# A two-layer graph network on one core: the first layer's two projections as one job of 15 products, with its small steps placed one by one

## The chip, the core and the metric

The kernel runs on one core of a Trainium2 chip. The metric is the device time of the whole kernel in microseconds (us), as the median of several runs. Beside the runs there is one profiled execution, from which all views of the profile come.

## The reference

`x` is (128 graphs, 64 nodes, 768 features) in float32, `adj` a mask of (128, 64, 64). There are two layers, and each ends in a layer norm over features with its input added. Cut to what matters:

```python
# layer 0: 12 heads of 64
h    = einsum('bnd,ade->bane', x, W)                     # one 768 x 768 projection
th   = tanh(h)
attn = leaky(th . w_src + swap(th . w_dst))              # one number a node and head each
attn = softmax(where(adj, attn, -999))
feat = elu(einsum('banm,bame->bane', attn, h) + b)
gate = sigmoid(x @ H_w.T + H_b)                          # a second 768 x 768 projection
x    = layernorm(x + gate * feat + (1 - gate) * x)
# layer 1: 6 heads of 128
q, k, v = x @ Wq + bq, x @ Wk + bk, x @ Wv + bv
ctx  = softmax(where(adj, q k^T / sqrt(128), -9e15)) v
x    = layernorm(x + ctx @ Wf + bf)
```

All 8192 rows of x pass the six 768 x 768 projections. Everything is computed in float32.

## The kernel before

**Tiles.** 128 rows (two graphs) are a tile, two tiles a pair; there are 32 pairs. `t0 = 2p` and `t1 = 2p + 1` are the tiles of pair p. Layer 0 and the values v of layer 1 are done pair by pair in a first stage (up to about 1480 us), queries, keys, attention and output in a second, by groups of two pairs. The second stage is the same before and after but for where in SBUF the weights of q and k lie.

**Products with fewer multiplications.** In the first stage a projection of a pair is a `Job` (L247): rows, inner dimension and columns are halved, and seven block products (1 to 7) replace eight, at the price of block sums. A product is three matmuls of 128 x 128 weights (rows of x, transposed) on 384 columns of the weight matrix (L270). Blocks of x are summed on GpSimd (`x_sums`, L1086, by `block_sums`, L232: four sums of 128x384), the weights' blocks once on VectorE (`weight_sums`, L213). `way_out` (L279) takes results out of PSUM: the first on a place of the output is a copy on ScalarE (h and v, L850, L879) or an addition of the bias on VectorE (gate, L866), later ones are additions on VectorE (L851, L867, L880). The second stage has the same idea with 15 products of 256-wide blocks (`WIDE`, L70), where the inner dimension and the columns are cut in three and the rows in two.

**PSUM.** There are eight banks of 128 x 512: three with tag `y`, three `z`, two `m`. A job's products use `y` and `z`; transposes and attention use `m`. A bank is given out again in turn, and its next matmul waits for the last read of what it held.

**Order.** The order is written out by hand. `TURN` (L121) lists the 21 products that PE does in a turn of a pair: `h` and `g` (gate) of pair p, `v` of pair p - 1, and `u`, the rest of v of pair p - 2. `FIRST`, `SECOND` and `THIRD_AT` are for the first three pairs, `LAST` for the end, where the products of q come in. All other work is attached to positions in the turn by `at` and `was` (L1119, L1123). `step` (L305) issues a product, then the `way_out` of the product before it; then come the acts of that position. Each engine works its own list in this order and waits only for data and buffers. SyncE starts all DMA transfers, in program order too.

**The steps of a tile in layer 0**, with their lines: `products` (tanh on ScalarE, times w_dst on VectorE, times w_src on GpSimd, L888 to L890); `terms` (sums over a head on VectorE, L897, then the dst terms go to DRAM as a 128 x 12 block, L899, and come back broadcast to 64 partitions, L902, as `dd`); `with_bias` (b is added to h on GpSimd, L913, then halves of h are sent across to other partitions by DMA as `hx`, L918); `logits` (L926), `leaky`, `masked` (L942 to L949), `exps`; `probs_by_nodes` (transposes through `m`, L966), `attend` (small matmuls, L987, with a column of ones for the sum), `features` (L1003, L1004); `gate_tanh` (ScalarE), `residual` (gate times x on GpSimd, L1017), `elu1`, `gated` (L1022 to L1029); `stats`, `normed` (the layer norm, L310: moments on VectorE, a power on GpSimd at L322, scale on ScalarE at L327, then the row spill to DRAM); `by_features` (transposes of the result), `value_sums` and `v`.

**Beside it** the generator `sum_weights` (L346) makes the sums of weight blocks for the second stage, from DRAM to DRAM: loads of 128x256, additions on GpSimd (L366), a store. Each item of a turn moves it on by one or two steps.

Of the kernel before, what the change touches and what calls it, by code (L numbers as in the profile page):

```python
# [24 lines left out]
EP = E0 + 2  # L25
# [21 lines left out]
WOVEN = [  # L47
    (0, 1), (1, 1), (0, 2), (1, 2), (0, 6), (1, 6), (0, 5),
    (0, 7), (1, 5), (1, 7), (0, 4), (0, 3), (1, 4), (1, 3),
]  # L50

FIRST = ["h1", "h2", "h5", "h6", "g1", "h7", "g2", "h4", "g6", "g5", "g7", "h3", "g3"]

FIRST_AT = {3: 0, 6: 10, 8: 3, 11: 8, 12: 12, 13: 12, 14: 13, 15: 14, 16: 14, 17: 14, 18: 15, 19: 19, 20: 19}
SECOND = [
    "h1", "G4", "h2", "g1", "g2", "h6", "h5", "h7", "g6", "h4",
    "g5", "g7", "h3", "g4", "g3", "H1", "v1", "v2", "v6", "v5", "v7", "H2",
]  # L60
SECOND_AT = {11: 10, 12: 13, 13: 13, 14: 14, 15: 14, 16: 15, 17: 16, 18: 18, 19: 19, 20: 20}
SECOND_OLD = {
    7.5: 12, 0: 7, 1: 8, 2: 8, 3: 9, 4: 10, 5: 11, 6: 12, 7: 12, 8: 13, 9: 14, 11: 15, 12: 15, 15: 16, 16: 17, 19: 19,
}

# [26 lines left out]
    ["u4", "u3"]  # L95
    + [f"q{n}" for n in (0, 1, 2, 3, 4, 5, 6, 8, 7, 9, 10, 11, 12)]
    + ["v1", "v2", "v6", "q13", "v5", "v7", "q14", "v4", "v3"]
)
LAST_AT = {7.5: 8, 3: 3, 4: 4, 5: 5, 6: 6, 7: 7, 8: 9, 9: 10, 11: 12, 12: 13, 15: 15, 16: 17, 19: 18}
# [21 lines left out]
TURN = [  # L121
    "h1", "h2", "u4", "u3", "h6", "g1", "h5", "h7", "g2", "g6", "h4",
    "h3", "g5", "g7", "v1", "v2", "g4", "v6", "g3", "v5", "v7",
]

THIRD_AT = {pos: max(int(pos) - 2, 0) for pos in [*range(len(TURN)), 7.5]}
TURNS = {
    0: (FIRST, FIRST_AT, {}),
    1: (SECOND, SECOND_AT, SECOND_OLD),
    2: (TURN[2:], THIRD_AT, THIRD_AT),  # L130
}
# [3 lines left out]
def kernel(  # L135
# [9 lines left out]
    hwT: bass.AP,  # L145
# [33 lines left out]
    dst_d = [dram.tile([P, H0], F32, name=f"dstd_{t}") for t in range(2 * NP)]  # L179
# [164 lines left out]
    bias_c = {k: load_cols(src, f"b{k}_c") for k, src in (("q", bq), ("k", bk), ("v", bv))}  # L344

    def sum_weights(pool):  # L346

        for key, src in (("q", wq), ("k", wk), ("f", wf)):
            for n, (_, blocks, *_) in enumerate(WIDE):
                if blocks[0][2] > 0 and len(blocks) == 1:  # L350
                    continue
                for kc in range(2):

                    def block(k, f):
                        r0 = (2 * k + kc) * P
                        return src[r0 : r0 + P, f * W2 : (f + 1) * W2]

                    acc = pool.tile([P, W2], F32, tag="wacc", name=f"wacc_{key}{n}_{kc}", bufs=1)
                    nc.sync.dma_start(out=acc, in_=block(*blocks[0][:2]))
                    for k, f, sign in blocks[1:]:  # L360
                        t = pool.tile([P, W2], F32, tag="wadd", name=f"wadd_{key}{n}_{kc}_{k}{f}", bufs=1)
                        nc.sync.dma_start(out=t, in_=block(k, f))
                        yield
                        yield
                        yield
                        G.tensor_tensor(acc, acc, t, ALU.add if sign > 0 else ALU.subtract)  # L366
                    if blocks[0][2] < 0:
                        assert len(blocks) == 1
                        yield
                        yield  # L370
                        yield
                        G.tensor_scalar(acc, acc, -1.0, None, ALU.mult)
                    yield
                    yield
                    nc.sync.dma_start(out=wide_d[key][n][:, kc, :], in_=acc)
                    yield
                    yield

    def wide_place(key, n):
        flat = weights[key].rearrange("p b k f -> p (b k f)")  # L380
        at = PLACE[n] * 2 * W2
        return flat[:, at : at + 2 * W2].rearrange("p (k f) -> p k f", k=2)
# [373 lines left out]
    with ExitStack() as ph, ExitStack() as ph_r:  # L756
# [13 lines left out]
        def load_x(p):  # L770
            ts = []
            for i in range(PAIR):
                t = sb.tile([P, D], F32, tag="x", name=f"x_{2 * p + i}")
                nc.sync.dma_start(out=t, in_=x[p, :, i, :])
                ts.append(t)
            return ts
# [14 lines left out]
        xTs[0] = sbr.tile([P, KC, PAIR * P], F32, tag="xT", name="xT_0")  # L791
        w0_w = weights["q"] = wpool.tile([P, 7, HK, HALF], F32, tag="wa", name="w0_wq")
        for kh, blocks in ((0, (B11,)), (1, (B21, T3, B22))):
            rows = slice(kh * HK, (kh + 1) * HK)
            nc.sync.dma_start(out=xTs[0][:, rows, :], in_=xT[0][:, rows, :])
            for block in blocks:
                load_block(w0, w0_w, block)
        hb_bc = load_rows(sbr, hb, D, "hb_bc")
        b01_bc = load_rows(sb, b0, E0, "b01_bc")
        hw_w = weights["k"] = load_weight(hwT, "wb", "hw_wk", (B11, B21, T3, B22))  # L800
# [3 lines left out]
        A[0], x_steps = sums_of(G, sbr, "sx", xTs[0], "x0")  # L804
        all_of(x_steps)
        t1, t2, t4, t3 = weight_sums(V, w0_w)
        all_of((t1, t2, t3, t4))
# [21 lines left out]
        def new_h(t):  # L829
            h = sb.tile([P, H0, EP], F32, tag="h", name=f"h_{t}", bufs=3)  # L830
            G.memset(h[:, :, E0:], 1.0)
            return h

        h_of = per_tile("h", new_h)
        gate_of = per_tile("gate", lambda t: sb.tile([P, D], F32, tag="gate", name=f"gate_{t}", bufs=3))
        v_of = per_tile("v", lambda t: sb.tile([P, D], F32, tag="v", name=f"v_{t}"))


        def h_job(p):
            def at(m, n):  # L840
                return h_of(p, m)[:, n * J0 : (n + 1) * J0, :E0]

            def as_heads(b):
                return b.rearrange("p (j e) -> p j e", e=E0)

            return token_job(
                f"h{p}",
                A[p],
                w0_w,
                lambda mn, b: S.copy(at(*mn), as_heads(b)),  # L850
                lambda mn, b: V.tensor_tensor(at(*mn), as_heads(b), at(*mn), ALU.add),  # L851
                lambda b: S.copy(at(1, 0), as_heads(b)),
            )

        def gate_job(p):
            def at(m, n):
                return gate_of(p, m)[:, n * HALF : (n + 1) * HALF]

            def bias(n):
                return hb_bc[:, n * HALF : (n + 1) * HALF]  # L860

            return token_job(
                f"g{p}",
                A[p],
                hw_w,
                lambda mn, b: V.tensor_tensor(at(*mn), b, bias(mn[1]), ALU.add),  # L866
                lambda mn, b: V.tensor_tensor(at(*mn), b, at(*mn), ALU.add),  # L867
                lambda b: V.tensor_tensor(at(1, 0), b, bias(0), ALU.add),
            )
# [14 lines left out]
        def products(t):  # L884

            h = st[t]["h"]
            th = sbr.tile([P, 2, D], F32, tag="th", name=f"th_{t}")
            S.activation(th[:, 1, :].rearrange("p (a e) -> p a e", e=E0), h[:, :, :E0], AF.Tanh)  # L888
            V.tensor_tensor(th[:, 0, :], th[:, 1, :], wsd[:, 0, :], ALU.mult)  # L889
            G.tensor_tensor(th[:, 1, :], th[:, 1, :], wsd[:, 1, :], ALU.mult)  # L890
            st[t]["th"] = th

        def terms(t):

            th = st[t].pop("th")
            sd = small.tile([P, 2 * H0], F32, tag="sd", name=f"sd_{t}")
            V.tensor_reduce(sd, th.rearrange("p s (a e) -> p (s a) e", e=E0), AX.X, ALU.add)  # L897
            st[t]["sd"] = sd
            nc.sync.dma_start(out=dst_d[t], in_=sd[:, :H0])  # L899
            dd = work(f"dd_{t}")  # L900
            for g in range(2):
                nc.sync.dma_start(  # L902
                    out=dd[g * N : (g + 1) * N, :],
                    in_=dst_d[t][g * N : (g + 1) * N, :]
                    .rearrange("m a -> (m a)")
                    .partition_broadcast(N),
# [3 lines left out]
        def with_bias(t):  # L910

            h = st[t]["h"]
# [3 lines left out]

            hx = sb.tile([P, J0, EP], F32, tag="hx", name=f"hx_{t}")
# [4 lines left out]
        def logits(t):  # L922
            sd, dd = st[t].pop("sd"), st[t].pop("dd")
            att = work(f"att_{t}")
            att3 = att.rearrange("p (a m) -> p a m", m=N)
            V.tensor_tensor(  # L926
                att3,
                dd.rearrange("p (m a) -> p a m", a=H0),
                sd[:, H0:].unsqueeze(2).to_broadcast([P, H0, N]),
# [50 lines left out]
        def attend(t):  # L980
            pT, h, hx = st[t].pop("pT"), st[t].pop("h"), st[t].pop("hx")
# [32 lines left out]
        def residual(t):  # L1014

            xp = st[t]["x"]
            G.tensor_tensor(xp, st[t]["gate"], xp, ALU.mult)  # L1017
# [6 lines left out]
        def gated(t):  # L1024

            ex, gate, u = (st[t].pop(k) for k in ("ex", "gate", "x"))
            V.scalar_tensor_tensor(ex, gate, 4.0, ex, ALU.add, ALU.mult)
            x1 = sb.tile([P, D], F32, tag="x1", name=f"x1_{t}")
# [4 lines left out]
        def stats(t):  # L1033
            next(st[t]["norm"])
# [327 lines left out]
```

## Time and profile before

| | |
|---|---|
| median of 3 runs | 2881.39 us (2880.11 to 2882.06) |
| profiled execution, span | 2888.2 us |
| granted TensorE clock, mean | 0.998 |
| VectorE, ScalarE, GpSimd busy | 67%, 37%, 45% of the span |
| DMA moved | 348.73 MB, mean 121 GB/s |
| first matmul | 7.67 us after the start |
| last pair's products of h end, queries begin | about 1480 us |

In the profile PE is TensorE's matmuls, PEld its weight loads, DVE VectorE, ACT ScalarE, POOL GpSimd and SP SyncE. A group's row has busy time and the mean duration of one instruction, then the idle time of the engine in front of it and what ended most of that. A row of waits has the waiting engine and what it waited for, then total us, times and the longest. A float32 matmul on 64 columns or more is in the records as two.

### The profile page before, as it was taken

How to read it: one execution, taken by the hardware profiler on the slowest of the kernel's cores; microseconds unless marked ns; L12 is line 12 of the kernel's file. 1: busy time of each engine (PE TensorE's matmuls, PEld its weight loads, DVE VectorE, ACT ScalarE, POOL GpSimd, SP SyncE). 2: the span in 40 equal slices, each digit the busy share in tenths (PEclk: the TensorE clock that was granted, in tenths of full speed). 3: DMA queues.
4: the chain of work that ended last, by engine and by line, in shares of the span. 5: the costliest groups of instructions: out<-in, count | busy, mean ns of one | idle time of the engine just before them, and what ended most of it. 6: DMA issues, size and time to landing. Idle time of an engine off the chain costs nothing.

```text
span 2888.2 us, 47874 instructions
## 1 busy us (share of the span) xinstructions
PE 2840.2 (98%) x18252; PEld 2075.9 (72%) x18252; DVE 1924.9 (67%) x3203; ACT 1061.2 (37%) x1896; POOL 1303.5 (45%) x1253
## 2 busy tenths in 40 slices
PE   8999999999999999999999999999999999999998
PEld 4565556666566666666668888888888888888886
DVE  7888888887888888777763545555544555554556
ACT  2444444444444444444433223333222333322332
POOL 3444445454444544343343445343545443444534
PEclk9999999999999999999999999999999999999999
DMA  5444444444445444333353434432323333233432
GB/s 182 132 154 145 140 150 143 159 148 151 141 142 162 135 155 142 105 116 108 121 195 96 122 91 111 111 92 84 77 79 111 111 104 95 68 84 94 111 88 74
DMA packets 322068, 348.73 MB, mean 121 GB/s; under 512 B 147888, under 2 KB 247216, under 8 KB 321840
## 3 DMA queue, kind: packets, MB, share of 16 engines
q1 hardware_dynamic: 321840, 345.66, 39.7%
q8 instruction: 146, 2.39, 0.4%
q14 instruction: 82, 0.67, 0.1%
HBM read 198.48 MB, written 122.29 MB: 111 GB/s over the span
## 4 chain that ended last, share of the span: by engine, by line
PE 80%; DVE 9%; DMA 4%; ACT 3%; issue 2%; POOL 1%; SPq 1%; POOLq 0%; DVEq 0%; ACTq 0%
PE z_k L447 9%; PE z_o L494 9%; PE z_q L447 8%; PE y_h L270 6%; PE y_g L270 6%; PE y_k L447 6%; PE y_o L494 6%; PE y_q L447 5%; PE y_v L270 5%; PE z_h L270 4%; PE z_v L270 3%; PE z_g L270 2%; PE cp L634 2%; PE sp L550 2%; PE x_g L270 2%
## 5 line engine op out<-in xcount | busy, mean ns | idle before, releaser
L574 ACT ACTIVATE sc<-sc 128x512 f32<-128x512 f32 x48 | 30.7, 639 | 616.9 <-DVE sc L571 616.9
L695 POOL TENSOR_TENSOR y<-y,bf_bc 128x768 f32<-128x768 f32 x64 | 114.7, 1817 | 295.1 <-DMA y<-x1d 265.5
L507 DVE TENSOR_TENSOR y<-y,z_o 128x256 f32<-128x256 f32 x320 | 127.4, 417 | 140.0 <-PE z_o L494 139.9
L494 PE MATMUL z_o<-wf,so 128*128 128x256 f32 x896 | 215.8, 383 | 2.3 <-DVE y L507 1.2
L447 PE MATMUL z_q<-xs,w_wq 128*128 128x256 f32 x896 | 213.5, 381 | 1.0 <-POOL xs L411 0.9
L411 POOL TENSOR_TENSOR so<-ctxT 128x256 f32<-128x256 f32 x224 | 160.5, 737 | 89.8 <-PE y_o L494 44.0
L447 PE MATMUL z_k<-xs,hw_wk 128*128 128x256 f32 x840 | 200.0, 381 | 0.0
L447 PEld LDWEIGHTS z_q<-xs,w_wq 128*128 128x128 f32 x896 | 168.7, 190 | 25.0 <-POOL xs L411 1.3
L494 PEld LDWEIGHTS z_o<-wf,so 128*128 128x128 f32 x896 | 167.2, 190 | 26.9 <-issue 2.0
L322 POOL TENSOR_TENSOR rs_b<-ve_b,minus_half 128x1 f32<-128x1 f32 x64 | 40.5, 632 | 312.7 <-DVE ve_b L320 311.9
L1017 POOL TENSOR_TENSOR x<-gate,x 128x768 f32<-128x768 f32 x64 | 120.1, 1878 | 135.1 <-ACT gate L1068 121.6
L890 POOL TENSOR_TENSOR th<-th,wsd 128x768 f32<-128x768 f32 x64 | 118.0, 1844 | 137.7 <-DVE th L889 137.7
L447 PEld LDWEIGHTS z_k<-xs,hw_wk 128*128 128x128 f32 x840 | 160.3, 191 | 22.1
L322 POOL TENSOR_TENSOR rs_a<-ve_a,minus_half 128x1 f32<-128x1 f32 x64 | 35.9, 562 | 307.3 <-DVE ve_a L320 307.3
L411 POOL TENSOR_TENSOR xs<-r,r 128x512 f32<-128x512 f32 x112 | 147.8, 1338 | 39.5 <-DMA r<-x1Td 22.5
L462 DVE TENSOR_TENSOR qT<-qT,z_q 128x512 f32<-128x512 f32 x96 | 65.9, 687 | 140.8 <-PE z_q L447 140.8
L270 PE MATMUL y_h<-w_wq,xT 128*128 128x384 f32 x384 | 136.5, 492 | 8.3 <-DMA w_wq<-in_w_dram 7.7
L462 DVE TENSOR_TENSOR kT<-kT,z_k 128x512 f32<-128x512 f32 x96 | 66.0, 687 | 114.9 <-PE z_k L447 112.9
L270 PE MATMUL z_v<-wv,sv_v 128*128 128x384 f32 x384 | 137.5, 494 | 1.0 <-DVE v L880 1.0
L270 PE MATMUL y_v<-wv,x1T 128*128 128x384 f32 x384 | 136.5, 492 | 1.2 <-ACT v L879 0.9
L270 PE MATMUL z_h<-w_wq,sx_x 128*128 128x384 f32 x384 | 137.5, 494 | 0.0
L270 PE MATMUL y_v<-wv,sv_v 128*128 128x384 f32 x384 | 134.9, 488 | 1.9 <-DVE sv_v L241 1.0
(165 smaller groups left out, 6907.7 us busy)
## 6 DMA issues: line engine op xcount, KB each, us to landing
x<-in_x_dram SPq DMA_DIRECT2D x64, 384.0 KB, 3.7
dd<-dstd SPq DMA_DIRECT2D x128, 192.0 KB, 3.4
x1d<-x SPq DMA_DIRECT2D x64, 384.0 KB, 2.6
x1Td<-x1T SPq DMA_DIRECT2D x32, 768.0 KB, 4.5
vd<-v SPq DMA_DIRECT2D x64, 384.0 KB, 2.9
r<-x1Td SPq DMA_DIRECT2D x96, 256.0 KB, 3.4
v<-vd SPq DMA_DIRECT2D x384, 64.0 KB, 2.3
y<-x1d SPq DMA_DIRECT2D x64, 384.0 KB, 5.7
```

What stands on the lines that cost most here:

```text
L270: T.matmul(to[:, : self.n], lhsT, rhs, start=kc == 0 and not more, stop=kc == HK - 1, skip_group_check=more,)
L322: G.tensor_tensor(rstd, ve, minus_half, ALU.pow)
L411: G.tensor_tensor(t, self.of(x[0]), self.of(x[2]), x[1])
L447: T.matmul(b[:, half * W2 : (half + 1) * W2], w[:, kc, half * P : (half + 1) * P], x[:, kc, :], start=half == kc == 0 and not more, stop=k ...
L462: V.tensor_tensor(at, at, b.rearrange("p (h t) -> p h t", h=2), ALU.add if sign > 0 else ALU.subtract,)
L494: T.matmul(b[:, :W2], x[:, kc, :], w[:, kc, :], start=kc == 0 and not more, stop=kc == 1, skip_group_check=more,)
L507: V.tensor_tensor(at, at, self.banks[path][:, :W2], ALU.add if sign > 0 else ALU.subtract)
L550: T.matmul(self.sp_[gr * N : (gr + 1) * N, (i * 2 + a) * N : (i * 2 + a + 1) * N], qT[:, 2 * self.f + a, at], kT[:, 2 * self.f + a, at], s ...
L634: T.matmul(self.cp_[a][e, at], self.v_[rows, i, gr, e], self.scT_[rows, at], start=True, stop=True,)
L695: G.tensor_tensor(y, y, pools["bf"], ALU.add)
L890: G.tensor_tensor(th[:, 1, :], th[:, 1, :], wsd[:, 1, :], ALU.mult)
L1017: G.tensor_tensor(xp, st[t]["gate"], xp, ALU.mult)
```

## The change

1. **h and gate are one job**, `Fifteen`, by the list `PRODUCTS`: the weight matrices stand side by side (768 x 1536), cut in three along the inner dimension and in three along the columns, the rows of a pair in two. Each of 15 products is two matmuls on 512 columns and goes to one of five accumulators ("paths", PSUM banks; 0 and 2 on `y`, 1, 3 and 4 on `z`). Reads of a bank: 16, of which the first on each of six places is on ScalarE, ten on VectorE. h and gate share one tile `hg` of 24 heads x 65 (four buffers), and the ones column is one wide instead of two.
2. **Sums of x**: ten of 128x256 on GpSimd instead of four of 128x384, each with a position of its own and one buffer (three pairs share one). Those of pair 0 are on VectorE but for three.
3. **Weights**: nine raw blocks of 128x1024 are loaded, 17 sums made from them on VectorE between the first products (`MADE`), one is a negated copy on ScalarE. q and k of the second stage come to lie in the same tile.
4. **The gate's bias** leaves the way out of PSUM and becomes a step on GpSimd, `gate_bias`.
5. **Terms**: src and dst terms stand in a tile of 32 columns, which VectorE transposes in 32x32 blocks (`V.transpose`); one store sends it, and the two broadcasting loads take heads as runs of 32 nodes. `send` and `fetch` have positions of their own, and so has the transfer of `hx` (`other_half`).
6. **Norm, loads and spills in steps**: `stats`, `power`, `normed`, `spill_rows`; `inputs` and `plus_one` by tile. `x1` is made in place of x. th has one buffer instead of two.
7. **Weight sums of the second stage** work on 128x512 at once, with counted rests between the steps.
8. **Positions**: a list `items` of all products of the stage, tables of fractional positions (`NEW`, `OLD`, `SUMS`, and ones for the first four pairs), with new steps placed behind the products that they need. Pairs 0 and 1 do their 15 products without values; v lags by up to two pairs.
9. The loads of the bias columns bq, bk, bv go from the start of the kernel to item 13.

The core of the diff:

```diff
-EP = E0 + 2
+EP = E0 + 1
+PRODUCTS = [
+    (0, (2, 0), [(2, 0, -1)]),
+    (3, (1, 1), [(0, 1, -1)]),
+    (1, (9, ALU.add, (1, 0)), [(1, 0, 1)]),
+    (0, (2, ALU.add, (0, 0)), [(2, 1, -1)]),
+    (1, (1, 0), [(0, 0, 1)]),
+    (4, ((0, 1), ALU.subtract, 3), [(0, 1, 1), (1, 1, 1)]),
...
+PRODUCTS[0] = (0, (3, ALU.add, 6), [(2, 0, -1)])
+BUFFER = {6: 6, 9: 9, 2: 2, 3: 3, 0: 0, 5: 5, 8: 8, 10: 0, 12: 5, 13: 8}
-TURN = [
-    "h1", "h2", "u4", "u3", "h6", "g1", "h5", "h7", "g2", "g6", "h4",
-    "h3", "g5", "g7", "v1", "v2", "g4", "v6", "g3", "v5", "v7",
-]
+TURN = "u6 a0 a1 u5 u7 a5 a3 u4 u3 a8 a6 a7 a2 a10 a9 a12 a4 a14 a11 v1 a13 v2".split()
+EARLY = (
+    "a0 a5 a1 a7 a3 a8 a6 a10 a9 a2 a12 a4 a11 a14 a13".split(),
+    "a0 a5 a3 a7 a8 a6 a1 a9 a10 a2 a12 a4 a11 a14 a13".split(),
...
+NEW = dict(tanh1=1, terms1=3.3, bias1=3.7, send1=6.3, hx1=4.6, fetch1=6.5, logits1=8.5, leaky1=10.5,
+    masked1=10.8, exps1=11, tanh0=1.6, terms0=3.3, bias0=3.4, send0=4.2, hx0=6.8, fetch0=4.6,
+    gbias0=3.7, gbias1=2.8)
+SUMS = dict(next6=2.1, next9=0.4, next2=2, next3=2.6, next0=2.7, next5=9.9, next8=5.9, own10=4.3, own12=5.8,
+    own13=1.6)
...
+        class Fifteen:
+            def __init__(self, p):
+                self.p, self.banks, self.written = p, {}, set()
+            def product(self, n):
+                path = PRODUCTS[n][0]
+                more = path in self.banks
+                if not more:
+                    tag = "y" if path in (0, 2) else "z"
+                    self.banks[path] = bank(tag, f"{tag}_a{self.p}_{n}", 3)
+                b, x = self.banks[path], A[self.p][n]
+                for kc in range(2):
+                    T.matmul(b, x[:, kc, :], wa[:, n, kc, :], start=kc == 0 and not more,
+                        stop=kc == 1, skip_group_check=more)
+            def way_out(self, n):
+                path, _, reads = PRODUCTS[n]
+                b = as_heads(self.banks[path])
+                for f, t, sign in reads:
+                    f = (0, 2, 1)[f]
+                    at = hg_of(self.p, t)[:, 8 * f : 8 * f + 8, :E0]
+                    if (f, t) in self.written:
+                        V.tensor_tensor(at, at, b, ALU.add if sign > 0 else ALU.subtract)
+                    elif sign > 0:
+                        S.copy(at, b)
+                    else:
+                        S.mul(at, b, -1.0)
+                    self.written.add((f, t))
...
+        x_sums(V, 0, (6, 9, 2, 3, 0, 5))
+        negated()
+        x_sums(G, 0, (8,))
+        made(0)
+        made(1)
...
-            th = sbr.tile([P, 2, D], F32, tag="th", name=f"th_{t}")
+            th = sbr.tile([P, 2, D], F32, tag="th", name=f"th_{t}", bufs=1)
...
-            nc.sync.dma_start(out=dst_d[t], in_=sd[:, :H0])
+            sdT = small.tile([P, 32], F32, tag="sdT", name=f"sdT_{t}", bufs=1)
+            V.transpose(sdT, sd)
+        def send(t):
+            nc.sync.dma_start(out=dst_d[t].rearrange("b x r -> (b x) r"), in_=st[t].pop("sdT"))
+        def fetch(t):
...
-                    out=dd[g * N : (g + 1) * N, :],
-                    in_=dst_d[t][g * N : (g + 1) * N, :]
-                    .rearrange("m a -> (m a)")
-                    .partition_broadcast(N),
+                    out=dd[g * N : (g + 1) * N, :].rearrange("p (c m) -> p c m", c=2),
+                    in_=dst_d[t][2 * g : 2 * g + 2, :H0, :].rearrange("c a r -> c (a r)").partition_broadcast(N),
...
+        def gate_bias(t):
+            gt = gate_of(t)
+            G.tensor_tensor(gt, gt, as_heads(hb_bc), ALU.add)
```

## The prediction

> **What bounds the kernel now.** I read the busy line of the page first, then the slices in stages, the distances between matmuls, what PE waits for, and last DVE and POOL by form in quiet turns.
>
> ```profile
> PE 2840.2 (98%) x18252; PEld 2075.9 (72%) x18252; DVE 1924.9 (67%) x3203; ACT 1061.2 (37%) x1896; POOL 1303.5 (45%) x1253
> ```
> PE is busy 98% of the span, so only what shortens its list, or makes it wait, moves the time. By stage (columns: us, busy of PE, PEld, DVE, ACT, POOL with counts, clock, DMA share, GB/s):
>
> ```profile
> 52.00:110.00 58.00, 48.25 (x335) 28.58 (x337) 48.82 (x69) 27.69 (x44) 23.05 (x17) 0.94 0.35 109
> ...
> 938.00:984.00 46.00, 45.79 (x247) 27.70 (x246) 37.43 (x55) 20.02 (x32) 20.95 (x20) 1.00 0.45 145
> ...
> 1257.00:1303.00 46.00, 46.00 (x275) 28.35 (x267) 35.96 (x56) 20.25 (x32) 17.92 (x16) 1.00 0.36 113
> ```
> After 110 us PE hardly waits; DVE is second, some four fifths busy. Layer 1, from 1480 us on, is left as it is. What PE pays is the distance between starts, not the row's mean, whose ends overlap. The timeline of PE in layer 0 and in layer 1:
>
> ```profile
> 1325.41 2.10 PE L270 MATMUL y_v<-wv,sv_v 128*128 128x384 f32 x6
> 1327.35 2.10 PE L270 MATMUL z_g<-hw_wk,sx_x 128*128 128x384 f32 x6
> ...
> 1560.11 1.89 PE L447 MATMUL z_k<-xs,hw_wk 128*128 128x256 f32 x8
> 1561.83 1.89 PE L447 MATMUL z_q<-xs,w_wq 128*128 128x256 f32 x8
> ```
> A float32 matmul is two records. A product of three 384-column matmuls takes 1.935 us (7.74 over four, 1325.41 to 1333.15), 322.5 ns a record; 256 columns take 215.8 ns (13.81 us over eight groups of 8). The slope is 0.834 ns a column.
>
> **The PE's list.** A pair's h and gate now take 14 x 1.935 = 27.09 us. After: 15 products of two 512-column matmuls, 60 records. 512 is the slope continued by 128 columns: 322.5 + 106.7 = 429.2 ns, an estimate; 1.717 us a product, 25.75 us a pair. Saved: 1.34 us a pair, 42.8 us over 32 pairs. Weight loads (190 ns a record) stay covered. A quiet turn is 45.39 us (z_h at 1302.71 and 1348.10), so it becomes 44.05 if nothing else is longer. The 65th instead of 66th column of av is nothing, and the values' products keep their price.
>
> **DVE.** From 1121 to 1439 us, seven turns, its rows sum to 37.7 us a turn. Rows that bear on the edits:
>
> ```profile
> L926 DVE TENSOR_TENSOR att<-dd,sd 128x768 f32<-128x768 f32 x14 | 22.6, 1617 | 5.6 <-DMA dd<-dstd 5.6
> ...
> L949 DVE TENSOR_TENSOR att<-att,mx 128x768 f32<-128x768 f32 x14 | 13.4, 959 | 0.5
> ...
> L851 DVE TENSOR_TENSOR h<-z_h,h 128x384 f32<-128x384 f32 x14 | 7.7, 550 | 0.0
> ```
> and from the page
>
> ```profile
> L462 DVE TENSOR_TENSOR qT<-qT,z_q 128x512 f32<-128x512 f32 x96 | 65.9, 687 | 140.8 <-PE z_q L447 140.8
> ```
> Ten additions of 384 columns from PSUM (three to h, seven to gate, 5.6 us) go; the new job has 16 reads, six first ones on ACT and ten on DVE at the L462 price, 6.9: +1.3. Logits read runs of 32 instead of steps of 12: between L926's 1.62 and L949's 0.96; the access is then nearest L949's, so -1.3 a turn (0 at the other end). Two transposes of 128x32: no row; the smallest tensor rows are 0.15 to 0.22, two-input 128x768 is 0.96; I take 0.2 each, +0.4. DVE's own work becomes 38.1 (83% of a turn before, 87% after).
>
> **ACT** gets six copies of 512 columns at about 0.59 (0.48 for 384, 0.84 for 768) for four of 0.48: +1.6 on 21.7 us a turn. Nothing, at half load.
>
> **POOL.** Its rows sum to 17.6 us a turn there. Four sums of 384 columns go (5.5 us); ten of 256 come, at 0.74 (the row of the 128x256 sums of so): +7.4. The gate's bias, two of 128x768 at 1.82 (row L1017): +3.6. Two small memsets: +0.2. Total 23.3. The weight sums, 126 adds of 256 columns before (about 107 us), become 63 of 512 at 1.34 (row of xs), 84 us, spread by their counted rests over about 23 turns: 3.7 a turn, so 27.0.
>
> This is what speaks against the change, because POOL and DVE hinder each other. The timeline of both at the start:
>
> ```profile
> 43.69 2.11 POOL L242 TENSOR_TENSOR sx_x<-xT 128x384 f32<-128x384 f32 x1
> ...
> 44.98 2.04 DVE L218 TENSOR_TENSOR wv<-wv 128x1152 f32<-128x1152 f32 x1
> ...
> 45.76 2.11 POOL L243 TENSOR_TENSOR sx_x<-xT,sx_x 128x384 f32<-128x384 f32 x1
> ```
> POOL's 384-column sum takes 1.00 us alone and 2.11 here, DVE's 1152-column one 1.35 alone and 2.04 here: they take turns. The Trainium skill, "SBUF — State Buffer", section "SBUF: two separate sides", has it that a DVE operation with two SBUF inputs and a GpSimd one that reads SBUF hold a shared port exclusively for a whole instruction. By the rule I add both: POOL 27.0, DVE's two-input rows 14.8 (the six of 128x768 a tile and the value sums), and the masked copy 2.2: 44.0 of 44.05 us in turns with weight sums. But the row of the masked copy has 1058 to 1092 ns in 64 runs, never stretched, so by the rows it is not part of it: 41.8. PE stays the longest by either, without slack by the rule, with 2.2 us by the rows; I go by the rows.
>
> What the queueing does to DVE: with weight sums (110 to 1030 us) POOL was 4.8 us longer a turn than without, and DVE 2.05 longer, 0.43 per us. So 5.7 more on POOL is +2.5 (40.6, 92% of a turn), and with weight sums about 42.2 (96%).
>
> **Waits in the steady turns.** The stage of 110 to 1030 us lost 12.7 us against 45.39 a turn, mostly at
>
> ```profile
> PE pTp L966 <- DVE rden L1003: 3.5, 5, 1.1
> PE pTp L966 <- DVE fo L1004: 1.6, 9, 0.2
> ```
> where a transpose waits for DVE to free the bank. A fuller DVE comes to this more often. A new place: path 0's bank is open from a0 to a13, and three banks go round among path 0, path 2 and the values, so the next a0 waits for a13's addition. Two products lie between, 3.65 to 3.87 us. On DVE, in front of that addition, stand logits, the reduction of 1.74 (which needs POOL's th product) and the transpose. Laid out from a11's end, a11's end + 2.9 for POOL, then 1.74 + 0.2 + 0.69, gives 5.5; a0 is due at 7.5. So 2 us are free, which one POOL operation in the way (1.3 to 1.8) nearly uses up. I take 0.8 us of waits a turn over the 28 steady turns, 22 us, 10 more than before; the ends are 0 (all positions fit: -13) and 2 (+43).
>
> New waits on POOL: the sums have one buffer each, so they wait for the pair's last product that reads it; behind them stand the gate's product and the norm's power, and DVE's shift waits for that. Positions leave four items or more between release and use (7 us), so 0 here; uncovered, one sum, 0.74. th and the transposed terms have one buffer too: the second tile's tanh waits for the first's reduction, some six items earlier, 0.
>
> **The start.** The first product began at 7.67, waiting for a weight block, and 13 were through at 36.47: 25.2 us of work, 11.3 lost. After, bias loads no longer go in front of x, but a0 needs all of x, five chained sums (0.42 each) and a negated block: x at about 5.2, negated weights at 7.7 (the loads ran at 380 GB/s when full). Then 17 weight sums of 1024 columns, 1.2 each on DVE (1.35 for 1152), stand in front of products: seven before the fourth one (18.0, 2 us of waiting), fourteen before the eighth (27.8, 2.9). All 15 through at about 41.6: 15.9 lost, +4.6. The window 52 to 110 lost 9.8 us in waits (5.0 on a norm, 1.4 on an exponential) and some 2 to a slow clock; after, pair 0's attention lies among pair 1's 15 products and more. I take -8 (-12 to +6). Start together: -3.
>
> **Rest.** At the end the row blocks for the queries are asked for in the turn's last item, three value products (5.8 us) ahead of q0; before, four products (7.7 us) ahead. A block's load took 6.7 us on the chain and its sum takes 1.34, so q0 may wait some 2 us, against 6.0 us of waits in 1439 to 1531 that the three products partly fill: +1 (-3 to +4). Splitting norm, copies, sending and fetching adds no operation. The copies of x and the row spills move on SP's queue only; SP waited 103.3 us in 64 fetches for the store, and logits only 24.1 for dd, with other DVE work as cover. A fetch has two runs a partition where it had one: I take 3.4 us to landing as now; at twice that, logits, and a13's addition behind it, come 3 us later, which is rival 2.
>
> **Sum.** -42.8 - 3 + 10 + 1 = -35. On the profiled span of 2888.2 that is 2853; the profile lies 7 us over the median of the runs (2881.4), so 2846 for the median.
>
> **Rivals.**
> 1. Positions fit and early pairs run full: -42.8 - 13 - 6 = -62, 2820. For it: in 1076 to 1439 us PE lost nothing with DVE at four fifths. Against: DVE gets fuller.
> 2. The bank of path 0, or the m banks, hold PE 1.5 us a turn: 42 of waits, 29 more than before: -16, 2866.
> 3. Slower: the shared port. Were collisions at random, each of 16 two-input DVE operations a turn would wait POOL's share (0.61) times half an operation (about 0.75): 7.3 us, where I have 4 to 5. If DVE's turn passes PE's, PE follows DVE. It decides from 46.1 us a turn, 2.1 over PE's list, where all is spent. At 47 in the 23 turns with weight sums and 45 in the other five: 69 + 5 - 13 = +61 on -45: +16, 2898. Against: before, collisions were little over half of random.
> 4. It does not do what it says: if 512 columns ran slower than the slope by over 5%, the saving would be gone. The two measured widths are on one line with 2.3 ns over; 3 in 100.
>
> **How the numbers follow.** Forecast 0.46 (2832 to 2858), rival 1 0.16, rival 2 0.18 (2858 to 2875), rival 3 0.17, rival 4 0.03 (no change). The range, 2822 to 2880, leaves out the best end of rival 1 and rival 3. 0.2% is 6 us, about what a measurement of this kernel can tell from no change: faster 0.79, same 0.05, slower 0.16.
>
> **What would show it.** In the profile after: starts of a products 1.72 us apart; DVE near 40 us in late turns, 42 with weight sums; POOL 23 and 27; turns of 44 to 45 us; the first product near 8 us. Wrong, if PE's waits name DVE's hg additions or features by over 2 us a turn, if DVE's two-input rows rise by half, or if POOL's sx stand in front of PE.

## The result and the profile after

Slower: 2906.26 us at the median (2904.64 to 2907.45) against 2880.75 for the kernel before, ratio 1.0089 [1.0074, 1.0103]. The profiled execution after lies on its median (span 2905.6), the one before lay 7 us over its own. So the spans differ by 17.3 us, the medians by 25.5; what follows accounts for the spans.

The busy line of the page after:

```profile
PE 2813.2 (97%) x17484; PEld 1926.9 (66%) x17484; DVE 1999.5 (69%) x3282; ACT 1105.0 (38%) x1961; POOL 1547.2 (53%) x1501
```

PE has less to do and a smaller share of a longer span: it waits. The timeline of PE in one quiet turn says how much of each (start, length, line):

```profile
1297.64 1.88 PE L939 MATMUL y_a<-wa,sx 128*128 128x512 f32 x4
1299.36 2.10 PE L334 MATMUL x_v<-wv,x1T 128*128 128x384 f32 x6
...
1344.95 2.10 PE L334 MATMUL x_v<-wv,x1T 128*128 128x384 f32 x6
...
1348.82 1.88 PE L939 MATMUL y_a<-wa,sx 128*128 128x512 f32 x4
1350.53 1.88 PE L939 MATMUL z_a<-wa,xT 128*128 128x512 f32 x4
```

A 512-column product takes 1.72 us from start to start, as the slope gave. But the turn, from one x_v to the next, is 45.59 us and not 44.05. Added up from the distances of all matmuls, from the first one to layer 1's first key product (k0), PE's own work fell from 1455.2 to 1412.4 us, by 42.8 as forecast, and the time lost between records rose from 62.6 to 126.3. (What is called lost between the short matmuls of attention is a choice; other choices move these differences by about 1 us.) By stretch:

| stretch of the span | lost before | lost after | difference |
|---|---|---|---|
| 0 to 200 us | 22.6 | 38.1 | +15.5 |
| 200 to 1400 us | 30.4 | 74.0 | +43.6 |
| 1400 us to k0 | 9.7 | 14.2 | +4.5 |
| k0 to the end | | | -3.6 |

With -42.8 that is +17.2. Some of the loss is a slower clock: up to k0 the granted TensorE clock stood at 0.50 for 23.9 us after and for 6.8 us before, each time in a wait of PE or soon behind one (its record begins 13 us into the span). At half speed that is at most 12 us against 3.4 (an estimate from these times). The waits of PE in 240 to 1440 us (total, times, longest), where before had 6 us in all:

```profile
PE y_a L939 <- POOL sd L988: 22.4, 22, 1.4
PE y_a L939 <- DVE hg L955: 7.1, 18, 1.7
PE av L1087 <- ACT pT L1067: 3.7, 3, 1.4
PE y_v L334 <- ACT v L970: 3.0, 2, 1.6
```

The first row is nearly one wait a turn, and its name misleads: a memset of eight columns that PE has no use for. The timeline of the place shows whom PE waits for:

```profile
1324.37 0.73 POOL L877 TENSOR_TENSOR sx<-xT,sx 128x256 f32<-128x256 f32 x1
...
1328.21 0.96 DVE L980 TENSOR_TENSOR th<-th,wsd 128x768 f32<-128x768 f32 x1
...
1328.79 3.60 PE L939 MATMUL y_a<-wa,sx 128*128 128x512 f32 x8
1329.09 0.95 DVE L1128 SCALAR_TENSOR_TENSOR ex<-hg,ex 128x768 f32<-128x768 f32 x1
1329.25 2.46 POOL L981 TENSOR_TENSOR th<-th,wsd 128x768 f32<-128x768 f32 x1 [4.15 <-DVE th L980]
...
1330.07 2.46 DVE L1130 TENSOR_TENSOR x<-ex,x 128x768 f32<-128x768 f32 x1
...
1332.45 0.67 DVE L955 TENSOR_TENSOR hg<-hg,y_a 128x512 f32<-128x512 f32 x1
...
1333.27 1.96 PE L939 MATMUL y_a<-wa,sx 128*128 128x512 f32 x4 [0.89 <-POOL sd L988]
```

The eight records at 1328.79 are a10 and a9; the product at 1333.27 is a12. a10 and a12 add into the same bank (path 2), and a10's sum has to be read (L955, to h and gate) before a12 adds to it. a10 was done near 1330.5. VectorE read it at 1332.45, since in its queue stood the subtraction for x1 (L1130), which took 2.46 us where it takes 0.96 alone. It overlaps GpSimd's product of tanh and w_src (L981, 1.81 alone, 2.46 here). The times fit one hold behind the other: VectorE's L1128 ends at 1330.04, GpSimd's product 1.67 later, at 1331.71, and x1 0.82 after that. (a12's own sum of x, the row at 1324.37, was done at 1325.10, so a12 did not wait for that.) GpSimd starts there, since it waited for VectorE's product of the same tanh (4.15 us idle, releaser L980), so the collision comes in every turn.

By form, in 1030 to 1440 us (count, then busy us and mean ns, then idle before): VectorE's x1 subtraction, then the logits, the masked copy and the mask's compare,

```profile
L1130 DVE TENSOR_TENSOR x<-ex,x 128x768 f32<-128x768 f32 x18 | 30.7, 1705 | 1.1
L1026 DVE TENSOR_TENSOR att<-dd,sd 128x768 f32<-128x768 f32 x18 | 27.0, 1499 | 28.2 <-DMA dd<-dstd 28.2
...
L1042 DVE COPY_PREDICATED_SCALAR att<-nadj,neg 128x768 f32 x18 | 19.4, 1078 | 8.2 <-ACT att L1036 8.2
L1179 DVE TENSOR_SCALAR nadj<-adj 128x128 uint8<-128x128 uint8 x9 | 15.3, 1706 | 0.0
```

1705 is the mean of one tile at 0.96 and the other at 2.46. Logits also wait for their fetched rows dd more than before (28.2 us of idle; 5.9 before), which is a second thread below.

### The profile page after: what moved, and what is told of

Same layout as the page of the kernel before. It is cut to its first block, busy times and chain, and to the rows that moved or that the text cites. A ratio compares the mean times of both kernels' runs of the same rounds, so it can differ in the third digit from the quotient of the medians.

```text
span 2905.6 us, 46458 instructions
## 1 busy us (share of the span) xinstructions
PE 2813.2 (97%) x17484; PEld 1926.9 (66%) x17484; DVE 1999.5 (69%) x3282; ACT 1105.0 (38%) x1961; POOL 1547.2 (53%) x1501
## 5 line engine op out<-in xcount | busy, mean ns | idle before, releaser
L939 PE MATMUL y_a<-wa,sx 128*128 128x512 f32 x1024 | 482.5, 603 | 45.0 <-POOL sd L988 23.9
L939 PEld LDWEIGHTS y_a<-wa,sx 128*128 128x128 f32 x1024 | 188.2, 191 | 255.8 <-issue 159.8
L1117 POOL TENSOR_TENSOR x<-hg,x 128x768 f32<-128x768 f32 x64 | 138.1, 2158 | 249.8 <-ACT hg L1191 249.8
L981 POOL TENSOR_TENSOR th<-th,wsd 128x768 f32<-128x768 f32 x64 | 135.9, 2123 | 213.9 <-DVE th L980 209.8
L510 PE MATMUL z_q<-xs,wa 128*128 128x256 f32 x896 | 213.0, 381 | 0.4 <-POOL x L1117 0.4
L474 POOL TENSOR_TENSOR so<-ctxT 128x256 f32<-128x256 f32 x224 | 159.8, 730 | 90.6 <-PE y_o L557 46.1
L510 PE MATMUL z_k<-xs,wa 128*128 128x256 f32 x840 | 198.5, 379 | 0.0
L939 PE MATMUL z_a<-wa,xT 128*128 128x512 f32 x384 | 185.5, 606 | 4.8 <-DVE wa L862 3.2
L510 PEld LDWEIGHTS z_q<-xs,wa 128*128 128x128 f32 x896 | 168.9, 190 | 24.1 <-POOL x L1117 0.8
L510 PEld LDWEIGHTS z_k<-xs,wa 128*128 128x128 f32 x840 | 159.5, 190 | 21.7
L955 DVE TENSOR_TENSOR hg<-hg,y_a 128x512 f32<-128x512 f32 x225 | 151.4, 674 | 24.0 <-PE y_a L939 20.2
L1026 DVE TENSOR_TENSOR att<-dd,sd 128x768 f32<-128x768 f32 x64 | 95.4, 1490 | 99.6 <-DMA dd<-dstd 99.6
L474 POOL TENSOR_TENSOR xs<-r,r 128x512 f32<-128x512 f32 x112 | 146.7, 1326 | 25.5 <-PE y_k L510 12.5
```

The lines of the kernel that those rows point to most:

```text
L474: G.tensor_tensor(t, self.of(x[0]), self.of(x[2]), x[1])
L510: T.matmul(b[:, half * W2 : (half + 1) * W2], w[:, kc, half * P : (half + 1) * P], x[:, kc, :], start=half == kc == 0 and not more, stop=k ...
L939: T.matmul(b, x[:, kc, :], wa[:, n, kc, :], start=kc == 0 and not more, stop=kc == 1, skip_group_check=more,)
L955: V.tensor_tensor(at, at, b, ALU.add if sign > 0 else ALU.subtract)
L1026: V.tensor_tensor(att.rearrange("p (a c m) -> p a c m", c=2, m=32), dd.rearrange("p (c a m) -> p a c m", c=2, m=32), sd[:, H0 : 2 * H0].un ...
L1117: G.tensor_tensor(xp, gate_of(t), xp, ALU.mult)
```

## The experiments

In all of them h and gate stay one job of 15 products. Ratios are to the kernel before, run beside it on the same chip; groups of kernels ran on different chips, so across groups compare the ratios. "Turn" is x_v to x_v.

**First theory: the order of PE's list at a12.** I put one more product between a10 and a12.

```diff
-TURN = "u6 a0 a1 u5 u7 a5 a3 u4 u3 a8 a6 a7 a2 a10 a9 a12 a4 a14 a11 v1 a13 v2".split()
+TURN = "u6 a0 a1 u5 u7 a5 a3 u4 u3 a8 a6 a7 a10 a2 a9 a12 a4 a14 a11 v1 a13 v2".split()
```

> The change with a10 put in front of a2 in the steady turn, so that two products instead of one lie between a10 and a12, which share path 2's bank. Theory (a12 may not write the bank until VectorE has read a10 out of it, and that read stands behind the stretched subtraction of x1): the wait of 1.05 us at a12 goes, a14 then waits some 0.6 more for a12's read, turns 45.6 to about 44.9, 2889 us. Rival (a12 waits for its sum of x on GpSimd, as the name in the row of waits says): the wait stays, 2906 us.

Measured 2914.35, 1.0115 [1.0100, 1.0130]. Neither came. In its waits of 240 to 1440 us,

```profile
PE y_a L939 <- DVE hg L955: 43.2, 26, 2.4
```

the wait at a12 is gone and a14 waits instead, 1.7 us in each turn, behind a12's read. To clear that I also moved the reduction of the terms behind a12's read (`terms1=3.3` to `5.1`):

> As the swap of a10 and a2, and the reduction of the terms of tile 1 moved behind the read of a12 on VectorE's queue (terms1 from 3.3 to 5.1). Theory: a12's and a14's waits both go, turns 44.2, 2873 us. Rival (GpSimd's sums bind): 2906 us. A third way: VectorE, 42 us of 45.6, turns late elsewhere, turns of 45, 2890 us.

2915.58, 1.0117 [1.0102, 1.0132], and the wait is at the transposes of x1, 40.2 us in 25 turns. As a cure the first theory fell: wherever PE's list gives room, VectorE's queue is as late at the next step. That a12 waits for a10's read stands: with one more product between them that wait was gone.

**The terms' round trip** put back alone (a store of 128x12, no transpose, logits in steps of 12):

> The change with the terms sent as before (a 128x12 block, no transpose, logits reading steps of 12), positions unchanged. By operation VectorE pays 0.56 more a tile in logits and 0.21 less for the transpose: +0.7 us a turn. Theory (VectorE's lateness sets the turn): 0 to +15 us on 2906. Rival (the new round trip itself is what made the change slower, with dd landing in 4.0 us instead of 3.4): 2890 us or less.

2908.16, 1.0085 [1.0070, 1.0100], as the changed kernel: this edit is worth nothing either way.

**Second theory: GpSimd's product holds VectorE at that place.** I left GpSimd's product of tanh and w_src out (`G.tensor_tensor(th[:, 1, :], ...)` in `products`), then for one tile alone.

> The change without GpSimd's product of tanh(h) and w_src (the src terms are then plain sums of tanh(h)): 3.6 us less a turn on GpSimd, order unchanged. Theory (GpSimd's product holds up VectorE's subtraction of x1 and with it the read of a10): the subtraction for tile 0 falls from 2.46 us to 0.96, a12's wait falls below 0.2, turns about 44.4, 2876 us. Rival (VectorE's queue is too long by its own work alone): the subtraction is short but a12 still waits 0.5 us or more, 2890 us or more.

> The changed kernel, with GpSimd's product of tanh and w_src left out for each pair's second tile only (its logits then lack w_src). Theory A, one place: this product (2.1 us on GpSimd) stands right in front of VectorE's subtraction for x1 of the pair before and stretches it from 0.96 to 2.46 us, and the reads of the accumulating bank queue behind that; without it nothing else holds that place. A: nearly the whole gain of leaving both out (36 us): 2870 to 2876, turns of 44.1 to 44.3 us, the wait at a12 gone. Theory B, load: VectorE and GpSimd share time in proportion to GpSimd's work anywhere; each tile's product is worth half: 2886 to 2892, turns near 44.8.

> The counterpart: GpSimd's product of tanh and w_src left out for each pair's first tile only (its logits then lack w_src); the second tile's stays where it is. A: 2898 to 2906, turns still 45.4 to 45.6, the wait of 1.05 us at a12 still there. B: 2886 to 2892, turns near 44.8.

| left out | us | ratio | turn | PE lost up to k0 |
|---|---|---|---|---|
| both tiles | 2870.39 | 0.9955 [0.9939, 0.9972] | 44.1 | 90.7 |
| second tile | 2880.37 | 0.9990 [0.9978, 1.0001] | 44.15 | 96.4 |
| first tile | 2909.87 | 1.0093 [1.0077, 1.0110] | 45.6 | 126.0 |

The same instruction, of the same 1.81 us on GpSimd where nothing holds it, is worth 1.4 us of a quiet turn at one place and nothing at the other. Its row without the second tile's:

```profile
L1131 DVE TENSOR_TENSOR x<-ex,x 128x768 f32<-128x768 f32 x19 | 18.2, 959 | 1.2
```

That is 0.96 us in every tile, with one such product less on GpSimd a turn; with the first tile's left out instead, x1 stays at 1705. So the place counts and not the load. (2880 is 4 us over what A expected: several steady turns stay long, up to 48.8 us, and the runs spread from 2870 to 2890.)

**The product on VectorE instead**, whole computation, second tile alone and then both (`V` for `G`):

> The whole computation again: the second tile's product of tanh and w_src is made by VectorE right behind its product with w_dst. VectorE gets 0.96 us more of its own a turn and loses the 1.5 us by which the x1 subtraction is stretched; GpSimd loses 2.1 us. A: 2872 to 2882, turns of 44.1 to 44.5. B: the half of the load goes but a turn's VectorE work rises: 2888 to 2898. A third theory, VectorE's own work is what counts and the hold does not: 0.96 x 28 on top of the changed kernel, 2930.

> The whole computation: both tiles' products of tanh and w_src are made by VectorE. A: as with the second tile alone, plus 0.96 us of VectorE work a turn in a place that has room: 2872 to 2886. B: GpSimd's 4.3 us a turn are gone for 1.9 us on VectorE: 2878 to 2888. Third theory: 2955.

2888.67, 1.0023 [1.0011, 1.0035], turns of 45.07; and 2938.78, 1.0192 [1.0177, 1.0207], turns of 47.0. Theory A's ranges were missed both times; the first number lies in theory B's, the second in none. The second tile's takes 0.5 us off the quiet turn, where leaving it out took 1.4: the other 0.9 is the instruction itself, now in front of the same read. The first tile's, which on GpSimd cost nothing, costs 1.93 us a turn on VectorE. The timeline of the kernel with both:

```profile
1318.01 0.96 DVE L980 TENSOR_TENSOR th<-th,wsd 128x768 f32<-128x768 f32 x1 [0.56 <-ACT th L979]
1318.06 2.46 POOL L1012 TENSOR_TENSOR hg<-hg,b_bc 128x768 f32<-128x768 f32 x1 [2.87 <-ACT th L979]
...
1319.01 2.32 DVE L981 TENSOR_TENSOR th<-th,wsd 128x768 f32<-128x768 f32 x1
...
1321.25 0.67 DVE L955 TENSOR_TENSOR hg<-hg,y_a 128x512 f32<-128x512 f32 x1
1321.98 1.98 PE L939 MATMUL y_a<-wa,sx 128*128 128x512 f32 x4 [1.66 <-DVE hg L955]
```

In front of a13 stands a11's read, and in front of that the moved product. It takes 2.32 us and not 0.96, beside GpSimd's addition of b (L1012), which ends at 1320.52, so 1.4 of the 2.32 us are again a hold, at another place. My A had said that this place has room; it has none.

**The same work at another place.** First I moved GpSimd's product for the second tile behind the sum for product 9 (so that it starts when a9 is done), the reduction behind a12's read (5.3), the bias behind the power (4.2) and the norm ahead of the reduction (16.05).

> The whole computation with the same instructions on the same engines as the changed kernel; in the steady turns GpSimd's product of tanh and w_src for the second tile is issued behind the row sum for product 9 (so it starts when a9 is done, under VectorE's reads, statistics and none of its two-operand work), the bias behind it goes to 4.2, the terms' reduction to 5.3 (behind the read of a12), and the normalization to 16.05 (ahead of the reduction). Theory A, one place: turns of 44.1 to 44.4 us, 2866 to 2878. Rival, VectorE's queue is too full wherever the steps stand and the wait moves again, to a14 or to the transposes of x1: turns of 45.2 to 45.9, 2895 to 2915.

2935.46, 1.0169 [1.0151, 1.0186]. Quickest turns 44.9, most of 47 to 48: the terms are reduced 1.7 us later, logits wait for dd (44.7 us in 18, 28.2 in the changed kernel), the exponentials and ScalarE's copies of v behind them, and PE for those.

Then I left the reduction where it was and moved both products with w_dst and w_src behind the x1 subtraction, and the bias to 4.2:

```diff
-            V.tensor_tensor(th[:, 0, :], th[:, 1, :], wsd[:, 0, :], ALU.mult)
-            G.tensor_tensor(th[:, 1, :], th[:, 1, :], wsd[:, 1, :], ALU.mult)
+            if not steady(t):
+                by_weights(t)
...
+            if steady(n1):
+                put(at_of[p, 7] + 2.9, do(by_weights, n1))
```

(`by_weights` holds the two lines; steady tiles are the second ones of pairs 4 to 30.)

> The whole computation with the changed kernel's instructions on their engines. In the steady turns the two products of tanh with its weights (VectorE's and, behind it, GpSimd's) are issued for the second tile behind VectorE's x1 subtraction of the first tile of the pair before, and ahead of the read of a10; GpSimd's product then lies under that read and the statistics, and the subtraction can run unheld; the bias on GpSimd follows the power (4.2). The terms' reduction, and so the logits' round trip, keep their place. Theory A (the hold of 1.5 us at that one place): a12's wait gone, a14's read not later than now, turns of 44.1 to 44.5 us, 2868 to 2880, below the kernel before. Rival (VectorE's queue has no room anywhere, each shift comes back at the next read or at the logits): turns of 45.2 us or more, 2895 to 2925.

2906.82, 1.0081 [1.0063, 1.0099]. Half of each came: many turns are of 44.4 to 44.9 us and a12's wait is gone, but others are of 46 to 49. In its waits of 240 to 1440 us, VectorE's and then PE's longest:

```profile
DVE att L1034 <- DMA dd<-dstd: 130.3, 52, 6.2
```

```profile
PE y_v L334 <- ACT v L970: 16.3, 11, 3.2
```

**Why the rows were late: SP's queue (theory Q).** The timeline of that kernel, terms, hx and bias alone:

```profile
1243.66 1.68 POOL L1020 TENSOR_TENSOR hg<-hg,b_bc 128x768 f32<-128x768 f32 x1
1244.34 0.21 DVE L1002 STREAM_TRANSPOSE sdT<-sd 128x32 f32<-128x32 f32 x1
1245.36 0.47 SPq L1027 DMA_DIRECT2D hx<-hg  x1
1245.92 0.55 SPq L1028 DMA_DIRECT2D hx<-hg  x1
1246.56 0.54 SPq L1006 DMA_DIRECT2D dstd<-sdT  x1
...
1248.29 1.29 SPq L1011 DMA_DIRECT2D dd<-dstd  x2
```

The terms are ready at 1244.55. Their store leaves at 1246.56, since SP has to issue the transfers of hx first and those wait for GpSimd's bias (done 1245.34). For the second tile, store after transpose is 2.0 us at the median of that kernel, up to 4.6; 0.3 in the changed kernel, up to 2.1. So I put these transfers behind the fetch (`hx1=4.6` to `6.7`): with the products behind the x1 subtraction, alone, with the bias at its old place, and with later stores of the weight sums (three products more ahead of `wide_d[key][n]`).

> The whole computation: the kernel with the products behind the x1 subtraction, and the second tile's loads of hx (which wait on SP for GpSimd's bias) issued behind the terms' store and fetch instead of ahead of them (4.6 to 6.7). Theory Q, SP's order makes the terms late: the turns of 46 to 49 us go, all near 44.4, 2868 to 2880. Rival, the transfers themselves are slow (4.2 us at the median to land, 3.5 before): turns as they were, 2898 to 2910.

> The whole computation: the changed kernel with the second tile's loads of hx issued behind the terms' store and fetch (4.6 to 6.7), nothing else. Theory Q and theory A together: the quiet turns stay at 45.6 (the hold at the x1 subtraction is still there), the long ones (47 to 51 us, some 14 us above the quiet in all) shrink: 2892 to 2901. If the queue's order does not matter: 2903 to 2908.

> As the first kernel of this group, with GpSimd's bias at its old place (3.7, ahead of the power). By theory Q the bias's place matters no more, once hx stands behind the terms: within 4 us of the first kernel, 2866 to 2882; if the power behind the bias holds the normalization, waits at the transposes of x1 and 2885 to 2900.

> As the first kernel of this group, with the stores of the stage-2 weight sums issued three products later, so that SP meets them when GpSimd's last addition is done (SP stood up to 15.7 us at such a store). Theory Q extended to these stores: what is left of long turns in 240 to 1030 us goes, 4 to 10 us below the first kernel. If they block nothing that is ready: the same within 4 us.

| kernel | us | ratio | PE lost, 200 to 1400 us |
|---|---|---|---|
| changed | 2906.26 | 1.0089 [1.0074, 1.0103] | 74.0 |
| hx alone | 2897.66 | 1.0051 [1.0036, 1.0066] | 63.4 |
| products behind x1 | 2906.82 | 1.0081 [1.0063, 1.0099] | 71.7 |
| both | 2861.37 | 0.9925 [0.9911, 0.9940] | 27.5 |
| both, bias at 3.7 | 2871.20 | 0.9959 [0.9945, 0.9974] | 37.4 |
| both, later weight stores | 2863.80 | 0.9935 [0.9920, 0.9950] | 28.8 |

Theory Q holds: hx alone takes the long turns away (one of 48.6 is left, the others are 45.6 to 45.9) and leaves the hold; the products alone, with the bias behind them, take the hold away and make the terms late; both together give 45 us and a kernel quicker than the one before, by a sum that neither gives alone (9 and 0 us by the medians, 11 and 2 by the ratios). It is 7 us below the range that I had written. The order of bias and power is worth 10 us more, not within the 4 that I had written. Later stores of the weight sums gained nothing. The timeline of the kernel with both, at the place shown above:

```profile
1332.36 0.96 DVE L1136 SCALAR_TENSOR_TENSOR ex<-hg,ex 128x768 f32<-128x768 f32 x1
1332.94 5.32 PE L939 MATMUL y_a<-wa,sx 128*128 128x512 f32 x12
1333.35 0.96 DVE L1138 TENSOR_TENSOR x<-ex,x 128x768 f32<-128x768 f32 x1
1334.22 0.95 DVE L989 TENSOR_TENSOR th<-th,wsd 128x768 f32<-128x768 f32 x1
1335.09 0.68 DVE L955 TENSOR_TENSOR hg<-hg,y_a 128x512 f32<-128x512 f32 x1
1335.26 1.82 POOL L990 TENSOR_TENSOR th<-th,wsd 128x768 f32<-128x768 f32 x1 [5.97 <-DVE th L989]
1335.69 1.01 DVE L1146 BATCH_NORM_STATS2 st_a<-x 128x6 f32<-128x384 f32 x2
```

a10, a9 and a12 run as twelve records without a gap. x1 takes 0.96; GpSimd's product lies beside a read of PSUM and the statistics, which it does not stretch, and takes 1.82 itself. The turn by engine (from, to and length, busy us with counts in the order PE, PEld, DVE, ACT, POOL; clock, DMA share, GB/s), first the changed kernel, then this one:

```profile
1299.36:1344.95 45.59, 44.55 (x224) 23.07 (x223) 39.61 (x57) 21.47 (x35) 25.99 (x25) 1.00 0.34 114
```

```profile
1259.36:1303.51 44.15, 44.15 (x224) 23.16 (x222) 36.76 (x57) 21.47 (x35) 24.96 (x25) 1.00 0.35 118
```

The same 57 instructions take VectorE 2.85 us less.

**The start.** In the first 200 us PE lost 15.5 us more than before. Its longest waits there in the changed kernel, but for that of the first product:

```profile
PE y_v L334 <- ACT v L970: 5.0, 1, 5.0
PE y_a L939 <- ACT hg L959: 4.3, 1, 4.3
...
PE z_a L939 <- DVE wa L862: 3.2, 1, 3.2
```

After such a wait records run slow for a while: the product of pair 2 that waited 4.3 us took 2.86 us for its four records, 1.88 in the steady turns. The granted clock is the reason; it is the third number from the right, here behind that wait and just after:

```profile
94.90:98.20 3.30, 3.30 (x5) 1.06 (x4) 2.44 (x7) 2.26 (x4) 2.78 (x5) 0.50 0.20 53
98.30:101.70 3.40, 3.16 (x14) 1.86 (x13) 1.24 (x2) 2.07 (x4) 0.84 (x1) 1.00 0.36 145
```

In the first 200 us the clock stood at 0.50 for 13.7 us, 6.8 us longer than in the kernel before; that is at most 3.4 of the 15.5 us. Three kernels were to take one or two of these waits away. The first moved pair 0's a7 behind a6 and its gating ahead of the reduction (`gated0=13.6` to `12.3`).

> The whole computation; only the start differs from the changed kernel: in pair 0 product a7 follows a6 (it waited 3.2 us for its weight sum), and the tail of pair 0's second half is gated right behind its elu step, ahead of the reduction and a weight sum on VectorE (the first product of pair 2 waited 4.3 us for a buffer of h and gate that this step frees). TensorE lost 38.1 us in the first 200 us of the changed kernel, 22.6 in the kernel before. Theory, the two waits are lost time of their own: 7 to 9 us come back with the slow records behind them, 2897 to 2900. Rival, the next wait takes their place: 2904 to 2907.

2907.59, 1.0075 [1.0058, 1.0093]: nothing gained. PE lost 39.7 us there instead of 38.1; a product waits 7.4 us for the weight sums instead of 3.2, two wait 4.3 together for first reads (one, 1.7, before), and the wait for the buffer shrank only from 4.3 to 3.0. Together with the first of the moved kernels,

> The edits of the two kernels above together, whole computation. If both theories hold their gains add: 2858 to 2870. If the start's waits only move, as the moved kernel alone; if the steady wait moves too, 2895 to 2910.

2928.98, 1.0154 [1.0139, 1.0169], 6 us below that kernel at the median, though in the profiles the time up to k0 differs by 1.7 only (the profiled execution of this one was its slowest). The third took the first row's wait away: in pair 3, pair 1's values are stored as soon as they are complete (13.5 instead of one product into the next turn), on top of the quickest kernel.

> The whole computation: the fastest kernel so far (the products behind the x1 subtraction, hx behind the terms), and in pair 3 the store of pair 1's values issued at 13.5, right behind their last addition, instead of one product into pair 4's turn. If that store is the cause, the wait of 5.0 us and the half-clock records behind it (about 2 us) go: 2853 to 2857. If ScalarE's place in the queue is late anyway (the exponentials ahead wait for VectorE) or another wait takes the time: 2859 to 2863.

2860.54, 0.9920 [0.9906, 0.9933], against 0.9925 [0.9911, 0.9940]: the same within the measurement, by its profile 3 us less. In its place stands

```profile
PE y_v L334 <- DVE sv_v L305: 4.1, 1, 4.1
```

a value sum behind the logits on VectorE. The start is a row of waits one behind the other. Which one leads it (the 17 weight sums on VectorE, the four buffers of hg, or the order of the four early pairs) stays open. It is also what keeps the kernel with both moves from the forecast: in the first 200 us that kernel loses 20 us more than the kernel before, in all the rest 3 us less.

## Why the prediction was wrong

- **PE's list**: right. 1.717 us a product, 42.8 us in all; and turns of 44.13 to 44.15 where nothing holds PE (44.05 forecast).
- **DVE's work**: right. 57 instructions take 36.8 us in a turn with few collisions (38.1 forecast); 39.6 in the changed kernel's quiet turns (40.6). **POOL**: 26.0 there against 23.3; its rows at their quickest sum to 22.3, so the forecast of the work was right, and 3.7 us are rows that stretch beside VectorE's.
- **Waits of the steady turns**: the step that failed. I took 0.8 us a turn, 22 us over 28 turns, 10 more than before. It was 1.5 us in the quiet turns (45.59 - 44.05), and with the long turns PE lost 43.6 us more than before in 200 to 1400 us. The "new place" that I laid out was the bank of path 0 between one turn's a13 and the next a0, with its 2 us of room. I did not lay out the banks within a turn: path 2 takes a8, a10, a12 and a14, each has to be read before the next adds to it, and between a10 and a12 there is one other product, 1.7 us.
- **How collisions were priced**: I spread them (0.43 us of VectorE per us of GpSimd), which gave VectorE's sum rightly and hid that one of them falls on the same instruction in each turn, in front of a read that PE waits for. Rival 3 had the mechanism and the sign (2898 against 2906) but the wrong point: it was to decide from VectorE's turn passing PE's, 46.1 us. It decided at 39.6 of 45.6, so that its number came near is luck. Of my signs of being wrong one came, and for one row alone: x1's mean rose from 983 to 1705 ns. Rival 2's size (1.5 us a turn at a bank) was right for another bank.
- **The rule on the shared port** (the Trainium skill, "SBUF — State Buffer", "SBUF: two separate sides") holds where I applied it: x1's 0.96 becomes 2.46 beside GpSimd's product. Summed over a turn, as I did, it said nothing of the loss; it has to be laid on the timeline.
- **Start**: -3 forecast, +15.5 measured. Pair 0's 15 products were through at 44.25 us, not at 41.6: 18.5 us lost against 11.3 before, +7.2 where I had +4.6. From there to 100 us the loss is 2.4 less than before, and in 100 to 200 us 10.7 more, where I had counted on early pairs running full (-8).
- **End**: +1 forecast for row blocks that q0 waits for; +4.5 measured up to k0, and it is another wait: PE stood 4.7 us for ScalarE's copy of v (L970), with the clock at 0.50 behind it, and 0.6 us in all for products of q. The -3.6 behind k0 lies in layer 1, which the change leaves alone; the clock of the kernel before stood at 0.50 for 3.4 us there, at most 1.7 of it, and the rest has no known cause. That the two make +0.9 is luck.
- **SP's order** I costed at nothing ("other DVE work as cover"). It is 9 to 11 us in the changed kernel: hx stands ahead of the terms' store.

In sum: 33.6 us too little in the steady turns and 18.5 at the start make up the 52 between -35 and +17 of the spans. By the medians it is 60 (2846 forecast, 2906 measured); the other 8 are that the profiled execution before lay above its own median.

## What to carry to other kernels

When a bank is read between the products that add to it, lay out product, read and next product in order of time, with all that stands before the read in its engine's queue: an engine that is 87% busy can hold PE each turn, at the one place where its queue is long. Two engines that block each other cost what their overlap delays, so move the pair apart (under reads of PSUM or statistics here) before moving work between engines. And after each such move look at the queue of the engine that issues transfers: one transfer that waits for a late engine holds all behind it.

## What was not expected of the hardware

- The mask's compare, 128x128 bytes with one tensor input, took 0.216 us at the median before and 1.69 to 1.71 in every steady turn of the changed kernel (row L1179), each time ending 82 to 90 ns after the end of GpSimd's product of gate and x (L1117), while the masked copy (L1042, 128x768) stayed at 1078 ns in both. It is one short row that is held, and the long masked one that is not. In the kernel with both moves the compare is held as well (1.70 to 1.71), without a wait of PE behind it.
- VectorE's reads of PSUM (L955, 643 to 690 ns) and its statistics (533 to 549 ns) had the same length with GpSimd beside them.
